# Second layer of a four-layer kernel: unordered scatters, both expert weights in one gather, GELU by eight tiles, maxima of two 64-query halves

## The chip, the cores and the metric

The kernel runs on one core of a Trainium2 chip. The metric is device time in microseconds (us) of one execution of the whole program; lower is better. The kernel before takes 1999.97 us in the median of 6 runs (1993.72 to 2006.95).

## The reference, cut to what matters

Four layers work on x of shape (2, 1024, 128), that is 2048 tokens of width 128. Each normalises x, computes an attention s and a feed-forward g from the same xn, and adds s*g. The change touches the second layer only:

```python
xn = _layernorm(x, axis=-1)
s = _L1_attn_ref(xn, W_qkv, W_o)        # 16 heads of width 8
g = _silu(_L1_ffn_ref(xn, gate_w, expert_w1, expert_w2, ln_gamma, ln_beta))
x = x + s * g

# attention: a key counts where |query - key| <= 32
mask = jnp.abs(idx[:, None] - idx[None, :]) <= half
scores = jnp.where(mask, einsum('bhqd,bhkd->bhqk', Q, K) / SCALE, -inf)
out = einsum('bhqk,bhkd->bhqd', softmax(scores), V)

# feed-forward: each token goes to one of 8 experts (128 -> 256 -> 128)
onehot = one_hot(argmax(softmax(x_flat @ gate_w.T)))
he = gelu(einsum('end,edh->enh', xe, expert_w1), approximate=False)
ye = einsum('enh,ehd->end', he, expert_w2)
out = layernorm(ye of the token's expert * top_val) * ln_gamma + ln_beta
```

## The kernel before

**Tiling.** The tokens are 16 tiles of 128 (NT=16), in four quarters of 512. The layer is written by `l1_layer` (L846), with two helpers: `Heads` (L457) for attention and `Routed` (L633) for the experts. `Weave` (L134) interleaves them by hand: `run(main, side, n_main, n_side)` advances the attention's generator and, in proportion, a side generator, and calls functions that are due some steps later. PE, DVE, ACT and POOL execute in the order in which this code issues (`manual_schedule`); the DMAs on SP are not in that list of engines.

**Attention.** There are 8 groups n: batch b = n//4, and four heads. Projections are split into three bf16 parts (`project_in`, L500), go to DRAM and come back as stacks of 72 rows for queries and keys (`load_stacks`, L539, 12 DMAs on SP), so that one matmul over 72 rows gives a product of near f32 exactness. `maxima(n)` (L903) finds each query's largest score: for every t of 8 (128 queries, a window of up to 192 keys) and each pair of heads it issues two matmuls that put the band mask into PSUM (L884, an identity times `band`) and two that add the scores (L893), into `sr`, and one DVE reduction (L910) of 128 x 384. After four t, `maxima_rows` (L556) splits the maxima into three bf16 rows, transposes them and writes them with three DMAs on SP into rows 72 to 74 of the query stack. `attend(n)` (L914) computes scores with keys on the partitions, the negative maximum added by those rows (75 rows), again with two mask matmuls and two products for a pair of heads (`st`, L884, L893), exponentiates on ACT (L940), and multiplies with the values (L623: four heads side by side in column tiles of 32, output `o1p`). `normalise` and `project_out` finish a group and a batch half.

While `attend(n)` runs, the side generator `ahead(n)` loads the stacks of n+2, runs `maxima(n+1)` and, in n=0 and 1, `project_in(2+n)`. From the third maxima step of n=2 on it takes one step of the experts per maxima step; in n=7, 16 steps.

**Experts.** `Routed.route` (L649) runs before the first maxima: gate matmuls (L657), a chain of DVE operations that counts tokens per expert and gives each token a slot; an expert's slots are padded to whole tiles of 128, 23 tiles in all (NS1). Then 16 scatters (L727), indirect DMAs of POOL, write the tokens' rows into `slots_in` in DRAM. They all write the same DRAM tensor, so each waits until the former has landed. `Routed.steps` (L733) is the generator:

- `load(i)` (L739): 64 KB of a slot tile from `slots_in` (L741, a plain DMA on POOL), and the gather of the first weights of the tile's expert (L744, indirect DMA on POOL, 128 rows of 1 KB), five tiles ahead;
- for each tile: transpose (L763), two matmuls of the tile before (L766, into `f1h`), a copy to `h` on DVE or ACT in turn;
- one GELU over all 23 tiles (L776), ACT, 128 x 5888;
- `load2(i)` (L746, L748): the gathers of the second weights, four to eight ahead; for four tiles each the second products (L786, `f1y`), a copy (L790) and a write to `slots_out` on SP (L791);
- 16 gathers (L796) that bring the tokens' rows back into the storage of `xnT`, two per step, and 11 empty steps;
- the layer norm with the expert's gate and the silu (L802 to L833), six steps per quarter, and `leave` (L838), which adds s*g to x.

The line by which a scatter or gather is issued, and the rates of the two generators:

```python
nc.gpsimd.indirect_dma_start(k.slots, self.at(self.pos, t), k.xn[:, t, :], None)   # L727
weave.run(attend(n, o), ahead(n), 16, 22 + 3 * (n < 2))
```

Of the kernel before, what the change touches and what calls it, by code (L numbers as in the profile page):

```python
# [456 lines left out]
class Heads:  # L457
# [5 lines left out]
    def __init__(self, k, ctx, weave, li, qk, v, o, bq=None, bk=None, bv=None, bo=None):  # L463
        nc, tc = k.nc, k.tc
        self.k, self.weave, self.li = k, weave, li
        self.wqk = k.wm(qk).rearrange("p (a c) -> p a c", a=2)
        self.wv, self.wo = k.wm(v), k.wm(o)
        self.bk, self.bv, self.bo = bk, bv, bo

        def pool(name, bufs, **kw):  # L470
            return ctx.enter_context(tc.tile_pool(name=f"a{li}{name}", bufs=bufs, **kw))

        self.big, self.fx, self.wk, self.ep, self.sp = (pool(n, c) for n, c in (("b", 1), ("x", 2), ("w", 2), ("e", 8), ("s", 3)))
        self.dr = pool("d", 1, space=bass.MemoryType.DRAM)
        self.p_s, self.p_t, self.p_o = (pool("p" + n, c, space=PSUM) for n, c in (("s", 3), ("t", 3), ("o", 2)))

        self.ident_h = self.big.tile([P, P], BF16, tag="ident_h", name=f"ident_h{li}")
        nc.vector.tensor_copy(self.ident_h, k.ident)

        self.v = self.big.tile([P, NT, H1 * self.VW + 32], F32, tag="v", name=f"v{li}")  # L480
        nc.gpsimd.memset(self.v, 1.0)
        self.scale = 1.0 / math.sqrt(DK)
        self.bq = None
        if bq is not None:
            self.bq = self.sp.tile([P, 1], F32, tag="bq", name="bq", bufs=1)
            nc.vector.tensor_scalar(self.bq, bq, self.scale, None, ALU.mult)
        self.q, self.kk = [], []
        for j in range(3):
            self.q.append(self.big.tile([KR, 4, S], BF16, tag=f"qs{j}", name=f"qs{li}{j}"))
            t = self.big.tile([KR, 4, S], BF16, tag=f"ks{j}", name=f"ks{li}{j}")  # L490
            nc.gpsimd.dma_start(
                t[KP:KR].rearrange("p h (a t) -> p (h a) t", t=P),
                k.ones_h[0 : KR - KP, None, :].to_broadcast([KR - KP, 32, P]),
            )
            self.kk.append(t)
        self.parts = [
            self.dr.tile([2, 3, P, S], BF16, tag=f"d{b}", name=f"parts{li}{b}") for b in range(B)
        ]

    def project_in(self, j):  # L500
# [4 lines left out]
        xf = self.fx.tile([P, 2, 512], F32, tag="xf", name=f"xf{u}")  # L505
# [71 lines left out]
    def normalise(self, n, c, po, o, then):  # L577

        k, nc, u, hg = self.k, self.k.nc, f"{self.li}{n}{c}", n % 4
        ou = self.wk.tile([P, 512], F32, tag="ou", name=f"ou{u}")  # L580
# [52 lines left out]
class Routed:  # L633
# [15 lines left out]
    def route(self):  # L649
# [75 lines left out]
        nc.vector.tensor_scalar(self.rows, tiles, lane, None, ALU.add)  # L725
        for t in range(NT):
            nc.gpsimd.indirect_dma_start(k.slots, self.at(self.pos, t), k.xn[:, t, :], None)  # L727
# [5 lines left out]
    def steps(self):  # L733
        k, nc, pool, hd = self.k, self.k.nc, self.pool, self.hd

        h = pool.tile([P, 2 * NS1 + 1, P], F32, tag="h1", name="h1")
        xs, w1, w2 = {}, {}, {}

        def load(i):  # L739
            xs[i] = hd.wk.tile([P, D], F32, tag="xs", name=f"xs{i}", bufs=6)  # L740
            nc.gpsimd.dma_start(xs[i], k.slots[i * P : (i + 1) * P, :])  # L741
            if i:
                w1[i - 1] = hd.wk.tile([P, FF1], F32, tag="ew1", name=f"ew1_{i - 1}", bufs=7)
                nc.gpsimd.indirect_dma_start(w1[i - 1], None, k.i["l1_w1"], self.at(self.rows, i - 1))  # L744

        def load2(i):  # L746
            w2[i] = hd.wk.tile([P, 2, D], F32, tag="ew2", name=f"ew2_{i}", bufs=6)
            nc.gpsimd.indirect_dma_start(  # L748
                w2[i].rearrange("p c d -> p (c d)"), None, k.i["l1_w2"], self.at(self.rows, i)
            )  # L750

        for i in range(5):
            load(i)
        yield
        for i in range(NS1 + 1):
            if i + 5 < NS1:
                load(i + 5)
            if i + 5 == NS1:
                w1[NS1 - 1] = hd.wk.tile([P, FF1], F32, tag="ew1", name=f"ew1_{NS1 - 1}", bufs=7)
                nc.gpsimd.indirect_dma_start(w1[NS1 - 1], None, k.i["l1_w1"], self.at(self.rows, NS1 - 1))  # L760
            ph = self.p.tile([P, 3, P], F32, tag="s", name=f"f1h{i}")
            if i < NS1:
                nc.tensor.transpose(ph[:, 2, :], xs[i], k.ident)  # L763
            if i:
                for c in range(2):
                    nc.tensor.matmul(  # L766
                        ph[:, c, :], lhsT=w1[i - 1][:, c * P : (c + 1) * P], rhs=h[:, 2 * i - 2, :], start=True, stop=True
                    )
            lo, hi = (0 if i else 2), (3 if i < NS1 else 2)
            copy_on(nc, i % 2, h[:, 2 * i - 2 + lo : 2 * i - 2 + hi, :], ph[:, lo:hi, :])  # L770
            yield
            if i % 3 == 2:
                yield
        for i in range(4):
            load2(i)
        nc.scalar.activation(h[:, 0 : 2 * NS1, :], h[:, 0 : 2 * NS1, :], AF.Gelu)  # L776
        for _ in range(4):
            yield
        for i0 in range(0, NS1, 4):
            n = min(4, NS1 - i0)  # L780
            for i in range(i0 + 4, min(i0 + 8, NS1)):
                load2(i)
            py = self.p.tile([P, 4, D], F32, tag="s", name=f"f1y{i0}")
            for i in range(n):
                for c in range(2):
                    nc.tensor.matmul(  # L786
                        py[:, i, :], lhsT=h[:, 2 * (i0 + i) + c, :], rhs=w2[i0 + i][:, c, :], start=(c == 0), stop=(c == 1)
                    )
            y = hd.wk.tile([P, 4, D], F32, tag="ye1", name=f"ye1_{i0}")
# [3 lines left out]
            )  # L793
            yield
        for t in range(NT):
            nc.gpsimd.indirect_dma_start(self.y[:, t, :], None, k.slots_out, self.at(self.pos, t))  # L796
            if t % 2:
                yield
        for _ in range(11):
# [46 lines left out]
def l1_layer(k):  # L846
    nc, tc = k.nc, k.tc
    half = WIN // 2
    with ExitStack() as ctx:
# [5 lines left out]

        zero = big.tile([P, KW], F32, tag="zero", name="zero1")
        nc.gpsimd.memset(zero, 0.0)
        nc.gpsimd.affine_select(
            out=zero, in_=zero, compare_op=ALU.is_ge, fill=-1e30, base=0, pattern=[[1, KW]], channel_multiplier=-1
        )  # L860
        band = big.tile([P, 2, KW], BF16, tag="band", name="band1")
        for i in range(2):
            nc.gpsimd.affine_select(
                out=band[:, i, :],
                in_=zero,
                compare_op=ALU.is_ge,
                fill=-1e30,
                base=2 * half,
                pattern=[[-1, KW]],
                channel_multiplier=1,  # L870
            )
# [6 lines left out]
        def scores(pool, tag, name, n, t, q, kk, i0, rows):  # L878
# [3 lines left out]
            ps = pool.tile([P, 2, KW], F32, tag=tag, name=name)  # L882
            for i in range(2):
                nc.tensor.matmul(  # L884
                    ps[:, i, 0:w],
                    lhsT=hd.ident_h,
                    rhs=band[:, i, m0 : m0 + w],
                    start=(i == 0),
                    stop=False,
                    skip_group_check=True,  # L890
                )
            for i in range(2):
                nc.tensor.matmul(  # L893
                    ps[:, i, 0:w],
                    lhsT=q[0:rows, i0 + i, t * P : (t + 1) * P],
                    rhs=kk[0:rows, i0 + i, w0:w1],
# [5 lines left out]

        def maxima(n):  # L903
            q, kk = hd.q[n % 3], hd.kk[n % 3]
            for c in range(2):
                nm = sp.tile([P, 4, 4], F32, tag="nm", name=f"nm1{n}{c}")
                for tt in range(4):
                    for i0 in range(0, 4, 2):
                        ps, _, w = scores(p_s, "s", f"sr1{n}{c}{tt}{i0}", n, 4 * c + tt, q, kk, i0, KP)
                        nc.vector.tensor_reduce(nm[:, tt, i0 : i0 + 2], ps[:, :, 0:w], AX.X, ALU.max, negate=True)  # L910
                        yield
                hd.maxima_rows(n, c, nm)

        def attend(n, o):  # L914
# [20 lines left out]
            for t in range(8):  # L935
                es = []
                for i0 in range(0, 4, 2):
                    ps, w0, w = scores(p_t, "st", f"st1{n}{t}{i0}", n, t, kk, q, i0, KR)
# [22 lines left out]
        moe = Routed(k, hd)  # L961

        def ahead(n):
            if n + 2 < 8:
                hd.load_stacks(n + 2)
            if n + 1 < 8:
                for i, _ in enumerate(maxima(n + 1)):
                    yield
                    if n > 2 or (n == 2 and i >= 2):
                        moe.step()  # L970
            if n == 7:
                for _ in range(16):
                    moe.step()
                    yield
            if n < 2:
# [9 lines left out]
        E = mybir.EngineType  # L985
        with tc.manual_schedule(engines={E.PE, E.DVE, E.Activation, E.Pool}):
            moe.route()
            weave.all(maxima(0))
            weave.flush()
            for n in range(8):  # L990
                if n % 4 == 0:
                    o = [hd.wk.tile([P, 4, H1, DK], F32, tag="o", name=f"o1_{n}{c}") for c in range(2)]
                weave.run(attend(n, o), ahead(n), 16, 22 + 3 * (n < 2))
# [785 lines left out]
def packed(a):  # L1779
# [14 lines left out]
    r["l1_w1"] = a["L1_ffn_expert_w1"].reshape(E1 * P, FF1)  # L1794
    r["l1_w2"] = a["L1_ffn_expert_w2"].reshape(E1, 2, P, D).transpose(0, 2, 1, 3).reshape(E1 * P, 2 * D)
# [75 lines left out]
```

## Time and profile before

| | |
|---|---|
| median of 6 runs | 1999.97 us (1993.72 to 2006.95) |
| profiled execution | 1998.93 us, of which the span from first to last instruction is 1997.2 us |
| PE busy, whole span | 1731.4 us (87%) |
| DVE, ACT, POOL busy | 1282.1, 825.5 and 586.8 us (64%, 41%, 29%) |
| granted TensorE clock, mean | 0.913 |
| second layer | about 1035 to 1341 us of the span |
| scores on PE into `sr` reduced on DVE, L910 | 128 times, 536 ns mean |
| exponentials on ACT, L940 | 128 times, 477 ns mean |
| scatters on POOL, L727 | 16 times, 960 ns median, from 1067.9 to 1132.4 us |
| GELU on ACT, L776 | once, 5111 ns |

Times are microseconds from the start of the span. PE is TensorE's matmuls, PEld its weight loads, which overlap them; DVE, ACT and POOL are VectorE, ScalarE and GpSimd; SP issues DMAs only. An engine's idle time is attributed to what released it, by semaphores. Where one line number stands for several uses (L884 and L893 serve the maxima and the attention), the tile's name tells them apart: `sr` is a maxima score, `st` an attention score, `o1p` the product with the values, `f1h` and `f1y` the experts' first and second products. In a table by stretches each row has the busy time of every engine within it.

### The profile page before, as it was taken

What the parts mean: (1) busy time and instruction counts of PE and PEld (TensorE: products, weight loads), DVE (VectorE), ACT (ScalarE), POOL (GpSimd) and SP (SyncE); (2) the same over time, 40 slices, a digit from 0 to 9 for tenths busy, and PEclk for the clock granted to TensorE, in tenths of its full rate; (3) what the DMA queues carried; (4) which work ended last, traced back from release to release, by engine and by line L of the source; (5) the groups of instructions that cost most, each with busy time, mean ns of one, the idle gap of its engine ahead of it and who ended that gap; (6) DMA issues with size and microseconds to landing.
All of it is one profiled execution on the core that took longest, in us unless ns stands there. A gap on an engine that the chain in (4) does not pass through costs nothing.

```text
span 1997.2 us, 24758 instructions
## 1 busy us (share of the span) xinstructions
PE 1731.4 (87%) x7884; PEld 924.0 (46%) x7884; DVE 1282.1 (64%) x2626; ACT 825.5 (41%) x1794; POOL 586.8 (29%) x908
## 2 busy tenths in 40 slices
PE   4999999999999999989976887665589939999997
PEld 2444444444444444434454576443366724444443
DVE  3988888888888888930025553578632463787771
ACT  1555555555555555432222432233113121466564
POOL 2233333333333333310031364211066351111211
PEclk9999999999999999999986988776689865899999
DMA  5333333333333333300004443120045223031200
GB/s 177 98 86 99 83 95 87 83 96 78 89 84 98 84 85 83 86 22 0 0 5 105 118 113 104 42 89 26 0 112 133 46 70 82 5 78 31 55 2 12
DMA packets 113618, 141.89 MB, mean 71 GB/s; under 512 B 26611, under 2 KB 98428, under 8 KB 110928
## 3 DMA queue, kind: packets, MB, share of 16 engines
q1 hardware_dynamic: 87520, 90.43, 17.4%
q0 software_dynamic: 25680, 49.84, 10.3%
q8 instruction: 64, 1.05, 0.2%
q14 instruction: 66, 0.54, 0.1%
q10 hardware_dynamic: 288, 0.03, 0.0%
HBM read 55.76 MB, written 16.78 MB: 36 GB/s over the span
## 4 chain that ended last, share of the span: by engine, by line
PE 54%; DVE 19%; DMA 9%; POOL 6%; issue 5%; ACT 4%; SPq 2%; another core or an unknown queue 1%; POOLq 0%; DVEq 0%; ACTq 0%
PE sc L261 10%; PE f0h L419 6%; PE pz L303 5%; DVE nm L271 5%; DMA aT<-tT 4%; PE o3p L623 4%; PE st L1568 3%; DVE e L281 2%; DVE tT L285 2%; PE po L321 2%; ACT e L273 2%; PE pq L237 2%; POOL aT L292 2%; PE sr L1530 2%; SPq L292 2%
## 5 line engine op out<-in xcount | busy, mean ns | idle before, releaser
L261 PE MATMUL sc<-xnT,q 128*128 128x512 f32 x1024 | 506.3, 596 | 6.4 <-ACT e L273 6.4
L273 ACT ACTIVATE e<-sc,nm 128x1024 f32<-128x1024 f32 x256 | 285.5, 1115 | 348.9 <-DVE nm L271 267.4
L271 DVE TENSOR_REDUCE nm<-sc 128x1 f32<-128x1024 f32 x256 | 307.8, 1206 | 9.3 <-PE sc L261 9.3
L261 PEld LDWEIGHTS sc<-xnT,q 128*128 128x128 f32 x1024 | 193.8, 191 | 234.5 <-issue 189.3
L292 POOL DMA_DIRECT2D aT<-tT x384 | 205.6, 542 | 323.6 <-DVE tT L285 177.6
L303 PE MATMUL pz<-aT,xn 128*128 128x512 f32 x512 | 262.6, 597 | 5.1 <-DMA aT<-tT 5.1
L1577 ACT ACTIVATE e<-st 128x512 f32<-128x512 f32 (+3 forms) x384 | 166.6, 492 | 122.1 <-PE st L1568 112.9
L281 DVE SCALAR_TENSOR_TENSOR e<-e,c,e 128x1024 f32<-128x1024 f32 x128 | 164.2, 1282 | 3.3
L285 DVE STREAM_TRANSPOSE tT<-e 128x1024 f32<-128x1024 f32 x128 | 158.4, 1238 | 1.9 <-DMA aT<-tT 1.1
L303 PEld LDWEIGHTS pz<-aT,xn 128*128 128x128 f32 x512 | 98.0, 192 | 121.4 <-issue 112.5
L71 POOL TENSOR_TENSOR f<-fv,neg_half 128x1 f32<-128x1 f32 x128 | 82.5, 645 | 201.2 <-DVE fv L335 144.1
L1538 DVE TENSOR_REDUCE nm<-sr 128x1 f32<-128x384 f32 (+3 forms) x176 | 106.5, 637 | 40.8 <-PE sr L1530 40.1
L940 ACT ACTIVATE e<-st 128x384 f32<-128x384 f32 (+1 forms) x128 | 59.2, 477 | 158.4 <-PE st L893 98.1
L1568 PE MATMUL st<-qs,ks 75*128 75x512 bf16 (+3 forms) x384 | 117.9, 331 | 1.0 <-ACT e L1577 0.9
L321 PE MATMUL po<-vc,z 128*128 128x384 f32 x256 | 105.8, 495 | 4.9 <-ACT oc L332 2.2
L419 PE MATMUL f0h<-h,hw 128*128 128x512 f32 x256 | 110.0, 592 | 0.0
L910 DVE TENSOR_REDUCE nm<-sr 128x2 f32<-128x384 f32 (+1 forms) x128 | 66.0, 536 | 47.9 <-PE sr L893 38.9
L1516 DVE TENSOR_REDUCE nf<-sf 128x1 f32<-128x512 f32 x128 | 82.2, 682 | 11.9 <-PE sf L1515 11.7
L623 PE MATMUL o3p<-e,v 128*32 128x512 f32 (+3 forms) x768 | 88.0, 508 | 0.0
L433 DVE TENSOR_TENSOR f0y<-f0o,bv 128x512 f32<-128x512 f32 x4 | 2.8, 692 | 121.3 <-PE f0o L429 121.3
L321 PEld LDWEIGHTS po<-vc,z 128*128 128x128 f32 x256 | 47.3, 191 | 71.7 <-issue 46.4
L419 PEld LDWEIGHTS f0h<-h,hw 128*128 128x128 f32 x256 | 48.6, 190 | 61.2 <-issue 61.2
(371 smaller groups left out, 2742.3 us busy)
## 6 DMA issues: line engine op xcount, KB each, us to landing
aT<-tT SPq DMA_DIRECT2D x640, 64.0 KB
aT<-tT POOLq DMA_DIRECT2D x384, 64.0 KB
w<-in_l_e SPq DMA_DIRECT2D x16, 768.0 KB
qs<-parts SPq DMA_DIRECT2D x144, 64.0 KB
ks<-parts SPq DMA_DIRECT2D x48, 192.0 KB
parts<-hm SPq DMA_DIRECT2D x16, 384.0 KB
w<-in_l_w POOLq DMA_DIRECT2D x8, 640.0 KB
hw<-in_l_h POOLq DMA_DIRECT2D x1, 2048.0 KB
```

What stands on the lines that cost most here:

```text
L261: nc.tensor.matmul(ps[:, n * 512 : (n + 1) * 512], lhsT=q[:, m, hf * 512 + t * P : hf * 512 + (t + 1) * P], rhs=k.xnT[:, b * S + n * 512 : ...
L271: nc.vector.tensor_reduce(nm, ps, AX.X, ALU.max, negate=True)
L273: nc.scalar.activation(em, ps, AF.Exp, bias=nm, accum_out=(s1, s2)[m][:, t : t + 1])
L281: nc.vector.scalar_tensor_tensor(e[0], e[1], c, e[0], ALU.mult, ALU.add)
L285: nc.vector.transpose(tT[:, :, t % 2, :, :].rearrange("p j J c -> p J j c"), e[0].rearrange("p (J j a) -> p J j a", J=8, j=4),)
L292: (nc.gpsimd if j == 3 or (i == 0 and j > 0) else nc.sync).dma_start(aT[32 * j : 32 * j + 32, t - 1 : t + 1, i, :, :].rearrange("a t J c - ...
L303: nc.tensor.matmul(pz, lhsT=k.xn[:, 8 * b + J, :], rhs=st["aT"][:, :, :, J, :].rearrange("p t i c -> p (t i) c"), start=(J == 0), stop=(J ...
L321: nc.tensor.matmul(po.rearrange("p a d -> p (a d)"), lhsT=st["z"][:, t * P : (t + 1) * P], rhs=mats[h][1].rearrange("p a d -> p (a d)"), s ...
L419: nc.tensor.matmul(ph, lhsT=hw[:, l, c, j * P : (j + 1) * P], rhs=cur[:, c, cols], start=(c == 0), stop=(c == 3))
L623: nc.tensor.matmul(po[32 * i : 32 * i + 32, c0:c1], lhsT=self.v[:, kt, vc : vc + 32], rhs=es[i], start=start, stop=stop, skip_group_check= ...
L1568: nc.tensor.matmul(ps[:, n0:512], lhsT=kk[0:KR, i, kt * P : (kt + 1) * P], rhs=q[0:KR, i, c * 512 + n0 : c * 512 + 512], start=not diag, s ...
L1577: nc.scalar.activation(e[:, n0:512], ps[:, n0:512], AF.Exp)
```

## The change

The change does this, all in the second layer:

1. **Scatters.** The 16 scatters are declared independent of each other; what reads `slots_in` is made to wait for all of them.
2. **Slot rows** are loaded eight tiles at a time (512 KB, three loads, `first`) on SP's queue, no longer one tile at a time on POOL's.
3. **Weights.** First and second weights of an expert lie side by side in one array (`l1_w`, rows of 2 KB) and come with one gather per tile (`weights`), 13 buffers, two tiles ahead.
4. **GELU and second products by eight tiles.** `h` holds eight tiles, with two buffers; the GELU of eight tiles follows one step after their last product, the second products three and five steps after it. `ye1` has one buffer.
5. **Output gathers** go out one per step, followed by 3 empty steps, not 11.
6. **Maxima.** Per t, one matmul of 512 columns puts the mask of four heads into PSUM, and for each head two matmuls of 64 queries by their 128 keys (96 at the ends) go into partitions 0 to 63 and 64 to 127; one DVE reduction of 128 x 512 gives four maxima. The attention's scores take their mask with one matmul of two heads.
7. **Masks.** `band` has one copy; `inner`, `first` and `last` (128 x 128) are made on POOL at the layer's start.
8. **Order.** `moe.route()` is issued ahead of the hand-written order, and expert steps are spread by a table: 2, 8, 11, 11, 11, 11, 12 and 16 steps in the groups n = 0 to 7.
9. **Room.** In this layer `ep` (the exponentials) has 5 buffers for 8, `xf` and `ou` one for two.

The diff, cut to its core:

```diff
-        self.big, self.fx, self.wk, self.ep, self.sp = (pool(n, c) for n, c in (("b", 1), ("x", 2), ("w", 2), ("e", 8), ("s", 3)))
+        self.big, self.fx, self.wk, self.ep, self.sp = (pool(n, c) for n, c in (("b", 1), ("x", 2), ("w", 2), ("e", 5 if li == 1 else 8), ("s", 3)))
...
         for t in range(NT):
-            nc.gpsimd.indirect_dma_start(k.slots, self.at(self.pos, t), k.xn[:, t, :], None)
+            i = nc.gpsimd.indirect_dma_start(k.slots, self.at(self.pos, t), k.xn[:, t, :], None)
+            for j in self.scattered:
+                k.tc.declare_no_dep(i.ins, j.ins, reason="no two tokens have the same slot")
+            self.scattered.append(i)
...
+        def first(a):
+            n = min(G, NS1 - a * G)
+            xs[a] = pool.tile([P, G, D], F32, tag="xs", name=f"xs{a}", bufs=2)
+            d = nc.sync.dma_start(
+                xs[a][:, 0:n, :], k.slots[a * G * P : (a * G + n) * P, :].rearrange("(t p) d -> p t d", p=P)
+            )
+            for i in self.scattered:
+                k.tc.add_manual_dep(
+                    d.ins,
+                    i.ins.name,
+                    mybir.DependencyInfo(mybir.DependencyClass.Sync, mybir.DependencyReason.DATA),
+                    reason="a slot's row may come from any of the scatters",
+                )
+
+        def weights(i):
+            if i < NS1:
+                w[i] = hd.wk.tile([P, 2 * FF1], F32, tag="ew", name=f"ew{i}", bufs=13)
+                nc.gpsimd.indirect_dma_start(w[i], None, k.i["l1_w"], self.at(self.rows, i))
...
+        def gelu(a):
+            n = 2 * min(G, NS1 - a * G)
+            nc.scalar.activation(h[a][:, 0:n, :], h[a][:, 0:n, :], AF.Gelu)
...
+        first(0)
+        first(1)
+        for i in range(2):
+            weights(i)
+        yield
+        for i in range(NS1 + 8):
+            if i % G == G // 2 and 2 <= (i + G) // G < (NS1 + G - 1) // G:
+                first((i + G) // G)
+            weights(i + 2)
+            if i <= NS1:
+                hidden(i)
+            if 0 < i <= NS1 and (i % G == 0 or i == NS1):
+                a = (i - 1) // G
+                late[i + 1] = [lambda a=a: gelu(a)]
+                late[i + 3] = [lambda a=a: second(a * G)]
+                late[i + 5] = [lambda a=a: second(a * G + 4)]
+            for fn in late.pop(i, ()):
+                fn()
             yield
         for t in range(NT):
             nc.gpsimd.indirect_dma_start(self.y[:, t, :], None, k.slots_out, self.at(self.pos, t))
-            if t % 2:
-                yield
-        for _ in range(11):
+            yield
+        for _ in range(3):
             yield
...
+        def maxima(n):
+            q, kk = hd.q[n % 3], hd.kk[n % 3]
+            for c in range(2):
+                nm = sp.tile([P, 4, 4], F32, tag="nm", name=f"nm1{n}{c}")
+                for tt in range(4):
+                    t = 4 * c + tt
+                    ps = p_s.tile([P, 4, P], F32, tag="s", name=f"sr1{n}{t}")
+                    m = first if t == 0 else last if t == 7 else inner
+                    nc.tensor.matmul(
+                        ps,
+                        lhsT=hd.ident_h,
+                        rhs=m[:, None, :].to_broadcast([P, 4, P]),
+                        start=True,
+                        stop=False,
+                        skip_group_check=True,
+                    )
+                    for i in range(4):
+                        for r in (0, P // 2):
+                            q0 = t * P + r
+                            lo, hi = max(q0 - half, 0), min(q0 + 3 * half, S)
+                            nc.tensor.matmul(
+                                ps[r : r + P // 2, i, lo - q0 + half : hi - q0 + half],
+                                lhsT=q[0:KP, i, q0 : q0 + P // 2],
+                                rhs=kk[0:KP, i, lo:hi],
+                                start=False,
+                                stop=(i == 3),
+                                skip_group_check=True,
+                            )
+                    nc.vector.tensor_reduce(nm[:, tt, :], ps, AX.X, ALU.max, negate=True)
+                    yield
+                hd.maxima_rows(n, c, nm)
...
+        MOE = (2, 8, 11, 11, 11, 11, 12, 16)
...
+        moe.route()
         with tc.manual_schedule(engines={E.PE, E.DVE, E.Activation, E.Pool}):
-            moe.route()
             weave.all(maxima(0))
...
-                weave.run(attend(n, o), ahead(n), 16, 22 + 3 * (n < 2))
+                weave.run(attend(n, o), ahead(n), 16, 8 * (n < 7) + MOE[n] + 3 * (n < 2))
```

`hidden(i)` does what the old loop did for a tile (transpose, first products of the tile before, copy), and `second(i0)` the second products of four tiles, their copy and the write to `slots_out`. `ahead(n)` takes the steps of `MOE[n]` evenly among the eight steps of `maxima(n+1)`.

## Prediction

> **What bounds the kernel now.** I read the page's 40 slices first: the second layer, about 1035 to 1341 us, is where PE's tenths, 9 in most of the first half, are 6 to 8, and POOL's reach 6. Then a table of busy time by the eight groups of heads n (columns: stretch, us, PE, PEld, DVE, ACT, POOL busy, PE clock, DMA share, GB/s), here n=2 to n=7:
>
> ```profile
> 1133.00:1165.00 32.00, 25.42 (x276) 20.55 (x273) 14.51 (x36) 9.88 (x22) 24.07 (x32) 0.84 0.53 131
> 1165.00:1198.00 33.00, 27.43 (x283) 21.63 (x282) 15.70 (x38) 10.44 (x22) 17.70 (x22) 0.84 0.43 112
> 1198.00:1266.00 68.00, 39.48 (x341) 31.46 (x335) 17.89 (x40) 15.36 (x21) 31.26 (x33) 0.80 0.32 89
> 1266.00:1283.00 17.00, 16.94 (x217) 13.07 (x217) 12.06 (x32) 7.63 (x18) 0.00 (x0) 0.90 0.35 73
> 1283.00:1309.00 26.00, 20.04 (x214) 15.26 (x212) 21.81 (x76) 7.88 (x17) 3.07 (x3) 0.80 0.01 3
> ```
>
> n=5 (1266 to 1283) has no expert work and PE is busy all the time: PE bounds a bare group, and from the first exp of n=5 to that of n=6 it lasts 14.8 us. By first exps the groups take 24, 21, 31.9, 33.3, 70.0, 14.8, 25.6 and 21.6 us. n=6 is bound by DVE (21.81 of 26, the experts' norm). The excess lies in n=2 to n=4, and no engine is full there. What waits, by the waits of this layer (sum, times, longest) and by its timeline (start, length, and in brackets the idle time before and its releaser):
>
> ```profile
> POOL slots_in L727 <- DMA slots_in<-xn,posi: 38.6, 10, 7.0
> ...
> PE f1h L763 <- DMA xs<-slots_in: 5.4, 1, 5.4
> ```
> ```profile
> 1210.94 0.85 PE L623 MATMUL o1p<-e,v 128*32 128x192 f32 x4 [5.57 <-ACT e L940]
> ...
> 1247.22 0.53 PE L623 MATMUL o1p<-e,v 128*32 128x192 f32 x4
> ...
> 1265.52 1.71 ACT L940 ACTIVATE e<-st 128x384 f32<-128x384 f32 x4 [16.34 <-remote]
> ...
> 1266.06 0.43 PE L884 MATMUL st<-band,ident_h 128*128 128x160 bf16 x2 [11.96 <-ACT e L940]
> ```
>
> The waits: the 16 scatters run one after another, to 1132.4, though at first only POOL waits; experts start in n=2, after them. The timeline's first line: PE waits 5.6 us behind the one GELU. Its others: from 1247.8 on PE and ACT stand for 12 and 16 us with nothing visible between them. In that time POOL issues its 16 output gathers back to back:
>
> ```profile
> L796 POOL DMA_INDIRECT xnT<-slots_out,posi x16: 943/947/948, 1242.8 to 1261.5; - x16
> L748 POOL DMA_INDIRECT ew<-in_l_w,rowsi x23: 945/949/950, 1182.6 to 1235.5; - x23
> L744 POOL DMA_INDIRECT ew<-in_l_w,rowsi x22: 985/992/1000, 1136.4 to 1180.1; - x22
> ```
>
> The trace's semaphore updates of PE say more. Of 2189 only some 50 come over 0.4 us after their matmul's end, nearly all in four stretches where POOL issues eight or more indirect DMAs 1.25 us apart (1180 to 1190, 1214 to 1223, 1226 to 1236, 1243 to 1262). There they come 1.43 us apart, or not at all (1252.2 to 1265.5), from about 4 us after the first issue to 2 or 3 us after the last. Gathers that alternate with plain DMAs of POOL (1.85 us a pair, 1136 to 1179), and scatters 2.5 us apart, delay none. I call this the freeze; its cause isn't visible. By the gaps it takes about 6, 12 (second and third together) and 18 us.
>
> **A page speaks against it.** The Trainium skill, SBUF — State Buffer, Who interferes with whom, holds that DMA never contends with a compute engine and that PE and ACT wait on nobody. This trace's 16.34 us differ; by the page alone the sum below would end near 47 us of gain instead of 32.
>
> **The experts' steps.** The excess over 14.8 us, less the experts' own PE work (0.56 us per tile for transpose and first products, 0.44 for the second, which only moves): n=2, 31.9−14.8−10×0.56=11.5; n=3, 33.3−14.8−12×0.56=11.8; n=4, 70.0−14.8−1.1−10.1−4 (project_out)=40. Together 63. What of this stays: the output gathers are still 16 in a row in n=4 (one per step, but a step on PE is shorter than 1.25 us), so their 18 us stay. The GELU's wait comes three times: 5.11×2048/5888=1.78 us plus two table loads of 1.28 is 4.3 on ACT instead of 7.7, so PE waits 5.6−3.3=2.3, say 2.5, times three 7.5. The rest, 63−18−7.5=**38 us**, goes: 23 loads L741 and 46 gathers on POOL become 3 loads on SP and 23 gathers (23×1.25=29 us of POOL, for 23×0.6+46×1.25=71), spread over n=0 to n=3, and the last ten come in fours as buffers free.
>
> **A new burst.** The scatters no longer wait for each other, and 13 buffers for weights are free at once: 16+13=29 indirect DMAs at 1.25 us, 36 us in a row, from 1068 to 1104. PE has nothing to do until 1077. If the freeze works there too, its cost lies between 0 (scatters apart cost nothing) and 28 us (PE at rest from 1077 to 1105, as from 1252 to 1265). At the pace of the second and third old burst, 1.43 us per completion: maxima(0) now has 8 `sr` and 2 transposes, and half of n=0 has 8 `st` and 4 `sr`, so 22 completions take 31 us where they took 11+12=23, or some 18 once the maxima are shorter; 8 to 13 us lost. I take **15 us**, a little above that pace, since one old burst of four stopped outright.
>
> The loads on SP wait for all scatters, about 1068+20+2=1090; queued behind them on SP are the q rows of maxima(1), due near 1105. The first 512 KB are due at hidden(0), the last step of n=0, also near 1105; before, PE waited 5.4 us for such a load, so 0 to 5, taken as 0. `ye1` with one buffer makes a DVE copy (0.67 us) wait for an SP write of up to 3 us, five times: 0 to 15, taken as 0, since the pairs lie two steps apart (about 2.5 us). `ep`, `xf`, `ou` with fewer buffers: e's five cover more than the 2 to 4 that are read at once; 0 to 3, taken as 0. The route outside the fixed order may let DVE start project_in earlier (it waited 2.6 us in line there): −2.6 to +2.6, taken as 0. The added masks, some 8 POOL operations of 0.34 us at most, lie in POOL's idle time before 1068, where it waits 17 us for L716; without that cover 3 us.
>
> **The norm.** It starts in n=5, not n=6, and ends earlier. n=6 and n=7 have 25.6+21.6−2×14.8=17.6 us of excess, under DVE's norm work; n=5 has 17−12=5 us of DVE free, and what is done there is gone from n=6: **4 us**, between 0 (the gathers land too late for n=5) and 5.
>
> **Maxima on DVE.** Two 128x384 reduces (0.548 each, L910) become one of 128x512; the nearest row is the page's 0.682 for such a reduce to one value (L1516). 0.41 saved 64 times is 26 us of DVE. Only where DVE or the chain PE to DVE decides does it count: n=6 (8×0.41=3.3) and maxima(0) (9.64 of 11 us busy; 2): **5 us**.
>
> **Maxima on PE.** Before, a t takes four masks and four scores of 192 columns at 0.083, 0.66 us. After: one mask of 512 columns, 0.22 at the same pace; a change of tile shape; 8 products of 64 queries by 128 keys. The nearest row for a change of shape is L884 to L623 and back: the last `st` to the first `o1p` takes 0.17 where two `st` lie 0.083 apart, and the last `o1p` group to the next mask 0.14 more than two groups need, together 0.23. The nearest row for half arrays side by side is L623, where four products of 32 columns take the time of one. If the two of a pair run together: 0.22+0.23+4×0.057=0.68, no change. One after the other: 0.91, 64×0.25=+16 us. If each waits for its own weights (PEld 0.11, then the product, 0.06): 0.22+0.23+8×0.17=1.8, +73 us. Below: scores use one mask instead of two, at most 2 records less in a pair, −5 us. I take **0**, since L623 is the only row with halves of the array.
>
> The Trainium skill, TensorEngine Tiling (Array Packing), Restrictions, says that column tiling turns off the fast load of weights, which speaks for the last of these ends. In this trace eight loads of column tiles (PEld L623) are done in 0.16 us together. By the page the loads would lie open and the sum would end near the slower rival below; by the row they don't.
>
> **Sum.** 38+4+5−15=32. The profiled execution took 1998.93 us (span 1997.2 and 1.7 around it), 1.04 below the median of the runs, 1999.97. 1998.93−32=1967; on the median's footing **1968 us**. About 0.3%, 6 us, is what a measurement can tell from no change.
>
> **Rivals.** *The early burst costs nothing*, as scatters 2.5 us apart cost nothing: 47 us gained, 1953. *It stops PE outright*: 28 for 15, 1981. *The halves run in line*: +16, 1984. *Ordering remains* (a scatter still waits for its forerunner, through a shared queue's count): then the loads come at 1135 as before, hidden(0) holds up PE from about 1107 to 1137, with no early burst, but 30 us of wait: 17 gained, 1983. *The slower end, one mechanism:* in maxima, each 64-column product waits for its weights on PE. PE is what bounds the bare group, so all counts: +73−32, about 2041; it decides from 0.5 us per t (32/64), that is if a t costs over 1.16 us on PE. For it speaks that PEld's 0.11 is longer than a product of 0.06, so the load can't hide; against it that L893's matmuls come each 0.083 with loads of 0.11 already.
>
> **Numbers.** The chances: forecast 0.38 (own range 1950 to 1978); no early cost 0.16; outright stop 0.12; halves in line 0.10; ordering remains 0.06; the slower one 0.12, from 1995 to 2050; two of the small costs together, about 1996, 0.06. The range, 1932 to 2010, leaves out about half of the slower case, and some of what both gains below would make together (no early cost, −5 on PE, −2.6 on DVE: 1945, and a sum that is itself 10 to 15 us too small). Faster 0.78, the first five cases (0.82) less 0.04 for their upper ends; same 0.07; slower 0.15.
>
> **What would show it.** Right: scatters 1.25 us apart after 1068, 512 KB loads on SP near 1092, the first f1h near 1105, three GELUs in n=1 to n=4, 23 gathers, the 12 to 18 us gap at the output gathers still there, groups n=2 and n=3 near 25 us, late PE completions between 1077 and 1107. Wrong: a group with 16 maxima steps and no experts above 15 us or PE's time per t above 0.7 (halves in line, or slower); no late completions early (the first rival); scatters still apart. What I can't exclude is that the freeze is a trait of the profiled execution, so that the plain times gain less than the spans.

## The result and the profile after

The changed kernel takes 2011.91 us in the median of 20 runs (2003.34 to 2023.29), the kernel before 1999.14 us over 46 runs. The ratio is 1.0063, 95% interval 1.005 to 1.0076: slower by 0.6%, where the forecast was 1968 us. The profiled execution took 2004.08 us, its span is 2002.4.

By first exponentials the groups n=0 to n=7 begin at 1114, 1145, 1174, 1212, 1240, 1279, 1296 and 1319 us; before it was 1089, 1112, 1134, 1166, 1199, 1269, 1285 and 1314. The standstill in n=4 is still there, n=2 to n=4 together are shorter by 30 us, but 40 were lost ahead of n=2. The table of busy time, with the same columns as before. First the kernel before, ahead of n=0 and in n=0:

```profile
1077.00:1088.00 11.00, 8.45 (x70) 7.15 (x67) 9.64 (x25) 0.00 (x0) 1.72 (x2) 0.80 0.34 77
1088.00:1112.00 24.00, 22.16 (x231) 16.56 (x229) 15.44 (x36) 10.29 (x21) 6.73 (x8) 0.86 0.38 103
```

Then the changed kernel, ahead of n=0 and in n=0, n=2, n=3, n=4 and n=5:

```profile
1088.00:1114.00 26.00, 5.01 (x37) 2.19 (x37) 6.11 (x16) 0.00 (x0) 11.43 (x12) 0.50 0.43 125
1114.00:1145.00 31.00, 29.52 (x219) 14.13 (x220) 11.17 (x23) 10.47 (x23) 0.00 (x0) 0.59 0.43 87
...
1174.00:1212.00 38.00, 31.30 (x320) 22.33 (x319) 15.30 (x36) 19.04 (x30) 8.91 (x10) 0.96 0.49 141
1212.00:1240.00 28.00, 25.95 (x290) 18.42 (x288) 13.16 (x31) 12.72 (x22) 0.57 (x1) 0.94 0.33 81
1240.00:1279.00 39.00, 24.59 (x235) 14.63 (x232) 11.04 (x26) 8.01 (x18) 15.13 (x16) 0.74 0.25 61
1279.00:1295.00 16.00, 16.00 (x217) 9.22 (x215) 10.65 (x32) 7.09 (x16) 0.00 (x0) 1.00 0.34 78
```

From 1088 to 1114 PE works 5 of 26 us and ACT none. Then n=0 has PE busy for 29.52 of 31 us, at a clock of 0.59; before, it took 23 us at 0.86. n=5, which has the new maxima and nothing of the experts, takes 16.2 us at full clock for 16.7 before. The timeline of the changed kernel's start says who waits:

```profile
1078.06 0.64 PE L950 MATMUL sr<-ks,qs 72*64 72x96 bf16 x8 [15.24 <-DMA ks<-parts]
...
1089.28 0.69 DVE L958 TENSOR_REDUCE nm<-sr 128x4 f32<-128x512 f32 x1 [6.37 <-remote]
...
1097.08 0.69 DVE L958 TENSOR_REDUCE nm<-sr 128x4 f32<-128x512 f32 x1 [7.12 <-remote]
...
1106.90 1.29 DVE L958 TENSOR_REDUCE nm<-sr 128x4 f32<-128x512 f32 x2 [8.28 <-remote]
...
1107.65 0.61 PE L938 MATMUL sr<-last1b,ident_h 128*128 128x512 bf16 x1 [8.67 <-DVE nm L958]
...
1266.65 0.87 ACT L1012 ACTIVATE e<-st 128x384 f32<-128x384 f32 x2 [11.59 <-remote]
```

DVE waits for scores that PE had finished: in the 24 us from 1082.9 to 1106.9 only two of the eight reductions of maxima(0) run, 0.69 us each. "remote" means that the profile saw no releaser. An engine reports a finished instruction by raising a semaphore, and the trace lists the time of each such update. Between 1078 and 1108 seven of the eight scores of maxima(0) are finished on PE and seven updates of PE arrive, so they can be paired in order. The fifth score is finished at 1084.1; its update comes at 1106.9, 22.8 us late, and its reduction starts there. Even the seventh, finished at 1099.0, is 8.1 us late. At 1266.5 the latest is 18.3 us late. The rows of indirect DMAs beside them, by tile:

```profile
L729 POOL DMA_INDIRECT slots_in<-xn,posi x16: 968/972/1017, 1067.1 to 1086.9; - x16
L763 POOL DMA_INDIRECT ew<-in_l_w,rowsi x23: 945/949/1112, 1065.7 to 1211.6; - x23
L835 POOL DMA_INDIRECT xnT<-slots_out,posi x16: 943/947/947, 1243.8 to 1262.5; - x16
```

The first 29 leave POOL 1.3 us apart, from 1065.7 to 1102.1. So the freeze of the prediction is where it was forecast, only harder.

### The profile page after: what moved, and what is told of

It is laid out like the page before. It is cut to its first block, busy times and chain, and to the rows that moved or that the text cites. A ratio compares the mean times of both kernels' runs of the same rounds, so it can differ in the third digit from the quotient of the medians.

```text
span 2002.4 us, 24516 instructions
## 1 busy us (share of the span) xinstructions
PE 1723.5 (86%) x7820; PEld 886.5 (44%) x7820; DVE 1260.5 (63%) x2561; ACT 830.3 (41%) x1803; POOL 554.0 (28%) x870
## 4 chain that ended last, share of the span: by engine, by line
PE 52%; DVE 20%; DMA 8%; POOL 6%; issue 5%; ACT 4%; SPq 2%; another core or an unknown queue 1%; POOLq 0%; DVEq 0%; ACTq 0%
PE sc L261 9%; PE f0h L419 5%; DVE nm L271 5%; PE pz L303 5%; DMA aT<-tT 4%; PE o3p L623 4%; PE st L1649 3%; DVE tT L285 2%; DVE e L281 2%; POOL aT L292 2%; PE po L321 2%; SPq L292 2%; ACT e L273 2%; PE pq L237 2%; PE sr L1611 2%
## 5 line engine op out<-in xcount | busy, mean ns | idle before, releaser
L958 DVE TENSOR_REDUCE nm<-sr 128x4 f32<-128x512 f32 x64 | 43.9, 689 | 99.5 <-PE sr L950 58.0
```

## The experiments

The theory: indirect DMAs back to back on POOL keep the completions of the other engines from arriving. The rivals: their volume does it; the new maxima are what costs. All times are medians, ratios are to the kernel before on the same chip.

**Paced.** A small fill of POOL (a memset of 0.26 to 0.28 us), twice behind each indirect DMA, makes them leave 1.7 to 2.0 us apart, the output gathers 1.73 (1.25 without). The scatters also move into the hand-written order here; the runs with less fill, further down, have that too. The edit, cut:

```diff
     nc.gpsimd.indirect_dma_start(...)
+    for _ in range(2):
+        nc.gpsimd.memset(zero, 0.0)
```

> The changed kernel with two fills of a small tile on POOL (some 0.6 us together) behind each scatter, weight gather and output gather, so that indirect DMAs leave POOL some 1.9 us apart and no longer 1.25; the scatters are issued inside the hand-written order. Theory (indirect DMAs back to back on POOL keep the completions of PE, ACT and DVE from arriving): the first exponential of n=0 comes near 1090 us and not at 1114, n=4 takes near 25 us and not 39.6, no idle time of 5 us or more without a visible releaser is left, and the kernel takes 25 to 45 us less than the changed one, about 1970. Rival (the volume of the gathers and of the 512 KB loads holds up the others, whatever the pace): n=0 begins at 1110 or later, and the time is that of the changed kernel within 6 us. Rival (the 64-query products cost the time): same time as the changed kernel within 6 us, n=0 earlier but each group longer.

1958.55 us, the kernel before 1973.44: 0.9915 (0.9883 to 0.9947). n=0 begins at 1093.6, n=4 takes 20.8 us, no update of PE is late. The numbers are those of the theory, but the kernel before is 26 us faster on this chip than in the first set of runs, so this run alone doesn't separate chip and pace.

**The maxima alone, the experts alone, ordered scatters**, on that same chip. The first is the kernel before with the new maxima. In the second, the maxima of before are put into the changed kernel; in the third, this goes from the changed kernel:

```diff
-            for j in self.scattered:
-                k.tc.declare_no_dep(i.ins, j.ins, reason="no two tokens have the same slot")
```

> The kernel before with the new maxima alone (masks of 128 columns, two products of 64 queries for each head, one reduction per t, one mask matmul for two heads of the attention's scores); experts, scatters and the order as before. Theory (the maxima cost PE nothing, 0.66 us per t before and after, and save DVE 0.41 us per t): 0 to 8 us less than before. Rival (the half-width products make the changed kernel slower): 10 us or more above before.

1974.61 us, 0.9989 (0.9965 to 1.0013): no difference. The maxima by themselves aren't the loss, though n=0 takes 29.6 us here, with the clock at half to 1110.7. One more thing is in this profile: n=4 has the indirect DMAs of the kernel before, 17 and 16 in a row 1.25 us apart, and takes 51.5 us where the first profile of before has 69.9, with no late update. So this chip shows no standstill with the old experts either, and that makes some 18 of the 26 us by which the kernel before is faster on it.

> The changed kernel with the maxima and masks of before (two pairs of heads per t, two reductions of 128 x 384, mask matmuls by head), and all edits of the experts kept. Theory (the loss lies in the burst of 29 indirect DMAs): n=0 begins as late as in the changed kernel, 1110 to 1118, and the time is 0 to 10 us above the changed kernel's. Rival (the maxima are the loss): at least 10 us below the changed kernel's.

1972.14 us, 0.9994 (0.9969 to 1.002). The profile is a surprise: indirect DMAs in rows of 9 and 18 at the start, 16 at the end, n=0 from 1097.5, n=4 in 21.2 us, and no late update at all. On this chip the standstill doesn't show in a profile. The theory's numbers for this run (n=0 from 1110 on) failed. The profiled execution, at 1962.84 us, is the fastest of the twelve, though, and 9 us under their median; what the slower ones lost isn't known.

> The changed kernel without the declaration that the scatters are independent: each waits for its forerunner again. The scheduler then puts the first weight gathers between the first scatters, in threes. Theory (back-to-back issue): the early standstill is gone or a few us, n=0 begins before 1095, but the slot rows are complete only near 1130 and PE waits for them in n=0 or n=1, 15 to 30 us; the time lies between 10 us under and 10 us over the changed kernel's. Rival (the gathers' volume holds up the others): n=0 begins at 1110 or later all the same and the wait for the slots comes on top, 15 us or more over the changed kernel.

1993.09 us, 1.0101 (1.0057 to 1.0146). The view of waits has the price of the order:

```profile
PE f1h L770 <- DMA xs<-slots_in: 30.3, 1, 30.3
```

Scatters to 1138.1, hidden(0) held up for 30.3 us, n=0 in 60.3 us. So independent scatters spare PE a wait of 30 us, once the experts begin in n=0; in the medians the ordered kernel lies 35 us over the paced one (1958.55) on this chip. On the standstill the run says nothing, as no profile of this chip has one.

**Again, on a chip where the kernel before takes 2000.88 us.**

> The changed kernel, unchanged, on the chip of the next three. The four runs before this one had the kernel before at 1973 us, not 1999, and no completion of PE came late in them, not even with 16 to 27 indirect DMAs back to back. Theory (the standstill depends on the chip, or comes and goes): where the kernel before takes near 1999 here, the standstill at 1082 to 1107 and 1252 to 1266 is back and the ratio is 1.006; where it takes near 1973, no late completions, and the ratio is 0.995 to 1.003. Rival (the standstill belongs to this program and is there on each chip): it is back whatever the kernel before takes.

2019.38 us, 1.0085 (1.0066 to 1.0104). Both standstills are back (n=0 from 1119.4, n=4 in 43.9 us; updates, paired in order, up to 25 us late), on a chip where the kernel before takes its longer time, as the theory had it. That it is the chip, and not the moment, isn't shown: the chip of the first four runs served in one set only, and the changed kernel as it is did not run there.

> The changed kernel with two fills on POOL behind each indirect DMA, and with the maxima and masks of before. Theory (the 64-query products keep PE's clock at half for longer: in the paced run with new maxima it was 0.5 from 1062 to 1116, in the kernel before only to 1081): the clock is back at full by 1090, n=0 takes 23 to 26 us and not 29.3, but n=6 takes 23 to 25 for 19.1 since DVE has more to do; in sum within 6 us of the paced kernel with new maxima. Rival (the clock stays low because PE waits before n=0, whatever the maxima): clock at half until 1110 again, n=0 near 29.

1964.14 us, 0.9802 (0.9778 to 0.9827), 55 us under the changed kernel on the same chip. No standstill. The clock is full from 1082.5 to 1089.3 and again from 1096.2, and n=0 takes 22.6 us, as the theory of the clock has it:

```profile
1092.00:1114.00 22.00, 19.85 (x222) 15.09 (x220) 13.34 (x31) 9.88 (x21) 18.54 (x38) 0.91 0.74 219
```

> The changed kernel with paced indirect DMAs, and 45 matmuls of 512 columns with no use for the result ahead of the first maxima, while PE waits for the stacks (from 1064 to 1078). Theory (what is lost in n=0 is the half clock): the clock is 1.0 from 1070 on and stays so, maxima(0) and n=0 together take 8 to 14 us less than in the paced kernel without them, n=0 near 22 us. Rival (the small products themselves bring the clock down again): the clock falls back to 0.5 within maxima(0) and n=0 takes 27 us or more.

1959.37 us, 0.9786 (0.9765 to 0.9807), 60 us under the changed kernel on the same chip. The warm matmuls bring the clock up, and it stays full through the 7 us of maxima(0) with the new products; it falls at 1084.8, about where PE then waits for 3 us, and is back only at 1112.2, late in n=0. Its table (warm matmuls and maxima(0), the wait, n=0):

```profile
1068.00:1085.00 17.00, 13.96 (x117) 6.59 (x115) 7.44 (x18) 0.00 (x0) 14.21 (x28) 1.00 0.58 140
1085.00:1088.00 3.00, 0.47 (x3) 0.27 (x3) 0.00 (x0) 0.00 (x1) 2.40 (x6) 0.50 0.11 37
1088.00:1118.00 30.00, 28.64 (x217) 13.87 (x217) 11.35 (x23) 10.33 (x22) 24.99 (x50) 0.60 0.68 185
```

PE is busy 28.64 of 30 us, and still the clock stays at 0.5 for the first 24 of them. The rival was right that n=0 takes 27 us or more, but not in its reason: here the clock fell with a pause and not within the new products, and n=0 was slow to lift it.

> The kernel before with two fills on POOL behind each gather of second weights and each output gather, nothing else. Theory on a chip with the standstill: n=4 takes 45 to 52 us and not 70, 15 to 25 us faster than before. On a chip without it: the same time as before within 5 us. Rival (the wait in n=4 belongs to the order of the experts' steps, not to the pace): n=4 takes 65 us or more where the unpaced kernel does.

1988.34 us, 0.9939 (0.9915 to 0.9962): 12 us, less than expected. The late updates all but go (none over 3 us), but n=4 takes 69.2 us as before, the number that the rival gave. The waits say why: its 17 gathers of second weights, now 2 us apart, hold up the second products.

```profile
PE f1y L791 <- DMA ew<-in_l_w,rowsi: 12.1, 12, 3.5
```

Before, PE waited for these weights 5 times, 4.0 us in all. So the fill gives with one hand and takes with the other there; what n=4 would take with neither wait, no run shows. In the paced changed kernel, with one gather per tile spread over n=0 to n=3, PE waits for no weights.

**Which row costs what**, on the third chip of these experiments, where the kernel before takes 2000.88 to 2001.62 us, as in all runs from here on.

> The changed kernel with the fills on POOL behind the 16 output gathers only; scatters and weight gathers back to back as in the change. Theory (each row of back-to-back indirect DMAs has its own price: 16 at the end some 20 us, 29 at the start some 30 us), on a chip where the changed kernel is slower than the one before: n=4 takes 21 to 24 us, n=0 still begins at 1112 or later, ratio to the kernel before 0.995 to 1.00, that is some 20 us under the changed kernel. On a chip without late completions: 0.992 to 1.0, no difference between this and the next run over 6 us. Rival (the standstill needs all rows together, some count of DMAs that runs full once): both standstills gone or both there.

1990.45 us, 0.9947 (0.9925 to 0.9969). n=0 from 1118.1, n=4 in 21.1 us.

> The changed kernel with the fills on POOL behind the scatters and the weight gathers only; the 16 output gathers back to back. Theory, on a chip where the changed kernel is slower than the one before: n=0 begins at 1088 to 1095, n=4 takes 39 us or more, ratio 0.985 to 0.992, some 35 us under the changed kernel. On a chip without late completions as in the run before. Rival: as there.

1982.17 us, 0.9911 (0.9882 to 0.9939). n=0 from 1091.0, n=4 in 39.3 us. Against 0.979 with all rows paced (the next run below, on the same chip, which has the maxima of before in n=0 and n=1), the start costs 0.9947−0.979=1.6%, 31 us, and the outputs 0.9911−0.979=1.2%, 24 us. The prices add up: 55 us together, where the run with the tiny fill (1.0074, the last of these experiments), in which both standstills are there, lies 57 us over 0.979. By the intervals each difference is good to some 6 us.

**The clock in n=0**, on the same chip as these two.

> The paced changed kernel with the maxima of before for the groups 0 and 1 only, the new maxima from group 2 on. Theory (the new maxima hold the clock at half in n=0, and spare DVE work where DVE bounds, in n=6): n=0 takes 22 to 24 us and not 29 to 30, the other groups as in the paced kernel, ratio to the kernel before 4 to 8 us better than the paced kernel's (0.979 on a chip with late completions, 0.9915 on one without). Rival (the lost time is only shifted, since hidden(0) waits for the slot rows, complete near 1105): n=0 shorter by 7 us but n=1 longer by as much.

1956.2 us, 0.979 (0.9767 to 0.9812). n=0 in 23.7 us, but n=1 in 32.0 for 29: no gain in sum over the paced, warmed kernel of the other chip (0.9786). Theory and rival were each half right. hidden(0) now comes before the slot rows (PE waits 2.3 us), and the clock is at half from 1114 to 1124.

> The paced changed kernel with each mask matmul of the maxima issued twice, the first one without use: 128 rows, 128 columns, 512 wide, 0.22 us more per t at full clock. It tells what keeps the clock at half. Theory (the clock gate wants more of the whole array's work than the half-width products give): the clock rises before 1100 and n=0 takes 24 to 28 us in spite of more work, n=1 to n=6 some 1.7 us longer each. Rival (the gate follows PE's busy share, or weight loads, whatever their width): n=0 takes 31 to 34 us with the clock at half to 1112 or later, and the kernel is 12 to 18 us over the paced one.

1969.31 us, 0.9853 (0.9828 to 0.9877). More work on PE, and n=0 is shorter, 25.6 us: the clock is full from 1100.5. First the paced kernel in n=0 (the first experiment, on its own chip), then this one:

```profile
1094.00:1123.00 29.00, 27.49 (x216) 13.58 (x217) 11.27 (x23) 10.09 (x23) 24.64 (x50) 0.62 0.71 201
```
```profile
1094.00:1120.00 26.00, 23.15 (x227) 11.88 (x228) 11.21 (x23) 10.35 (x22) 22.24 (x45) 0.88 0.82 215
```

Busy share 95% there, 89% here, and here the clock rises. With the maxima of before it rose earlier still (at 1082.5, and after a fall at 1089.3 again at 1096.2). So a busy PE was not enough here. Work of the whole array may be what counts, but the added matmuls are also the longest, with 512 columns, and no run separates the two; what lifts the clock stays open.

**The pace, more finely.** Two explanations of the paced runs are left: a limit of pace, or the lack of an instruction in between.

> The changed kernel with one fill on POOL behind each indirect DMA, not two: by the durations in the runs with two, indirect DMAs leave some 1.43 us apart (1.73 with two, 1.25 with none). Theory (the pace decides; each indirect DMA takes about 1.43 us where the completions queue behind it): no standstill, single completions late by up to 2 us, n=0 begins at 1086 to 1096 and n=4 takes 20 to 25 us; within 6 us of the run with two fills, ratio 0.976 to 0.984 on a chip with late completions. Rival (a limit at some higher pace, between 1.43 and 1.73): standstills of 10 us or more at the start and in n=4, ratio 0.99 or more.

2003.05 us, 1.0006 (0.9988 to 1.0024). The DMAs left 1.39 us apart, not 1.43. The standstill is milder at the start (n=0 from 1105.2, updates up to 9.6 us late), and nearly whole in n=4 (42.1 us, up to some 10). So 1.39 us is still too close: the rival, a limit at a wider spacing, was right against the theory's 1.43 us.

> As the run with one fill, with the maxima of before in the groups 0 and 1. Theory (with two fills the slot rows came too late for n=1, once the clock in n=0 was mended): the last scatter is 5 us earlier, n=0 takes 23 to 24 us, n=1 27 to 29 and not 32, and the kernel is 4 to 8 us faster than the one with two fills and these maxima; ratio 0.973 to 0.977 on a chip with late completions. Rival (the work of n=1 is what takes the time, or the clock falls again there): n=1 takes 31 us or more, ratio 0.979 as before.

1999.3 us, 0.9987 (0.997 to 1.0004). The standstill covers the question: n=0 34.2, n=1 32.0 us. It can't tell why n=1 is long.

> The changed kernel with a tiny fill (128 x 8) behind each indirect DMA: another POOL instruction stands between two of them, but they leave 1.2 to 1.35 us apart. Theory (the pace decides): both standstills are there as in the changed kernel, n=0 begins at 1110 or later, n=4 takes 38 us or more, ratio 1.00 to 1.01 on a chip with late completions. Rival (an instruction in between is enough): no standstill, ratio near 0.98.

2016.7 us, 1.0074 (1.0046 to 1.0102), 1.26 us apart, n=0 from 1117.8, n=4 in 43.9 us. An instruction in between is no help. The pace decides. The waits on "remote" of the run with one fill, the three longest, then those of the tiny one; with two fills behind all of them there is no such line:

```profile
DVE nm L967 <- remote: 26.5, 6, 9.3
ACT oTs L609 <- remote: 9.5, 1, 9.5
ACT e L1021 <- remote: 5.3, 1, 5.3
```
```profile
DVE nm L967 <- remote: 35.6, 5, 15.5
ACT e L1021 <- remote: 24.8, 2, 20.9
DVE rs L590 <- remote: 4.9, 1, 4.9
```

On this chip the limit lies between 1.39 and 1.73 us per indirect DMA of 128 rows; on the chip of the second set ("Again") only 1.25 us, with the standstill, and 1.73, without, were tried. What it is that these DMAs share with the semaphore updates, and why the chip of the first four runs shows no late update, none of the runs shows.

## Why the prediction was wrong

The step that failed is "A new burst": 15 us taken between 0 and 28, where the start alone cost 28 to 31. The row it was taken from (updates 1.43 us apart) was the mild form, seen in bursts of eight; 29 in a row give the hard form, as the 16 output gathers did. The mechanism was right and its size wrong. The rival with the outright stop had the price right, 28 us; but at 1981 it missed the time too, because the forecast's other terms held gains that weren't there. Term by term, in us, on the chip of the second set, from "Again" on (changed kernel 2019, paced ones 1959 and 1964, before 2001; from single profiles, so each is an estimate, good to 2 or 3 us):

- **Early burst**: 15 taken, 31 measured (n=0 from 1119.4 with it, from 1088.0 paced and warmed and from 1091.5 paced with the old maxima; from 1088.4 in the kernel before with its late gathers paced). Off by 16, or by 13 from 1091.5.
- **The clock**: the term "Maxima on PE", taken as 0, was priced at full clock. In n=0 the new maxima leave the clock at half: 30.0 us, 22.6 with the old ones (paced). 7.
- **Base of a group**: 14.8 was a misreading; from the first exponential of n=5 (1268.6) to that of n=6 (1285.3) it is 16.7. The excess of n=2 to n=4 was thus 57, not 63. 6. (n=6 was misread too: 28.5, not 25.6.)
- **The last standstill**: 18 said to stay, 22 do (43.9 for 21.6). 4. Two bursts of four gathers in n=2, "as buffers free", cost 5 more (39.5 for 34.1).
- **GELU and steps**: 7.5 taken to remain; over base and own work 9.7 remain in n=2 and n=3 (34.1 and 27.5, for 16.7 plus 11.5 and 16.7 plus 7.0) and 3.4 in n=1 (29.1, for 21.2 plus 4.5). 6 too few.
- **Norm and DVE**: 9 taken. n=6 and n=7 together take 43.5 paced, 44.8 before: 1, so 8 short. n=7 takes 19.1 to 19.4 in each variant of the changed kernel and 16.3 before, and n=6 between 19.1 and 26.0, with the clock; why n=7 grew stays open.

That makes 16+7+6+4+5+6+8=52 against a gain of 32: some 20 us slower, and 18.5 were measured there. With seven terms of 2 or 3 us uncertainty each, so close a sum is in part luck.

What was right: unordered scatters and gathers fall where they were said to; the maxima cost PE nothing at full clock (n=5 16.2 for 16.7; a mask 0.32 and eight products 0.34 us per t, 0.66 as before, by the starts below), so the slower rival with its 73 us never came; ordered scatters hold up hidden(0) by 30 us; the freeze is not a trait of the one profiled execution, since pacing takes 55 us off the medians of all runs.

```profile
1284.08 0.39 PE L938 MATMUL sr<-inner,ident_h 128*128 128x512 bf16 x1
1284.40 0.41 PE L950 MATMUL sr<-ks,qs 72*64 72x128 bf16 x8
1284.74 0.39 PE L938 MATMUL sr<-inner,ident_h 128*128 128x512 bf16 x1
```

What was wrong besides: the 512 KB loads, forecast near 1092, leave SP at 1122.0, and the first product into `f1h` comes at 1135.1, not 1105. The loads stand in SP's queue behind the rows of the late maxima, for which that queue waits up to 28.1 us (L573 on `nr`). In the paced kernels they leave at 1101 to 1104, and where hidden(0) comes soonest PE waits 2.3 us for them. n=2 and n=3, forecast near 25 us, take 38.2 and 27.5, paced with the new maxima 34.1 and 25.8 to 27.5.

The rule that spoke against the freeze (the Trainium skill, SBUF — State Buffer, Who interferes with whom: DMA never contends with a compute engine, PE and ACT wait on nobody) fits the one chip without late completions (ratio 0.9994 unpaced). On the two others late completions of 18 to 27 us speak against it as the prediction used it, for whatever a DMA can hold up. The section argues from ports of the memory, and no run here shows that a port is what the DMAs and the semaphore updates share. The rule that spoke for the slower rival (the Trainium skill, TensorEngine Tiling (Array Packing), Restrictions: column tiling turns off the fast load of weights) shows no cost in the 0.34 us for eight products.

The best versions are paced ones: 0.9786 (0.9765 to 0.9807) and 0.979 (0.9767 to 0.9812) to the kernel before, by the medians 0.97 of the changed one (1959.37 for 2019.38 on one chip). The change gains some 2% there, and 0.85% on the chip without late completions (0.9915), once its DMAs are kept apart.

## What to carry to other kernels

Indirect DMAs in a row can have a price for the other engines that no row of their own shows, here 24 to 31 us a row: look at when semaphore updates arrive, not only at when instructions end, and count what a removed wait will send out at once. A wait that paces a queue may be worth keeping; where it goes, put something in its place, and measure the spacing. Half-width matmuls were free here at full clock and cost 7 us after a pause: read the granted clock of that stretch before pricing.

## What the runs showed of the hardware that was not expected

- Late completions: up to 27 us after the end of the matmul, paired in order (the run with the tiny fill: score finished at 1081.5, update at 1108.8, reduction at 1108.9), with 16 to 29 indirect DMAs 1.25 to 1.3 us apart on POOL; up to some 10 us at 1.39; none over 2 us at 1.7 or more. On the two chips of the later sets, and in the first set; on the chip of the first four runs, none in profiles with up to 18 in a row at 1.25, though the unpaced runs there scatter more (1962.8 to 1976.8, paced 1955.8 to 1961.7).
- The clock stayed at 0.5 for the first 24 us of a group with 64-column maxima, with PE 95% busy in it, and rose 6 us after n=0's start once each 512-column mask matmul was issued twice.
